# A graph attention kernel: layer 1's transposes and last product in two one-bank PSUM buffers, and the first tile's x multiplied while its rows arrive

## The chip, the cores and the metric

The kernel runs on one core of one Trainium2 chip. Its time is device time in microseconds, as the median of several runs. A profile, taken by the hardware profiler in an execution of its own, gives start and duration of every instruction. TensorE is called PE, VectorE DVE, ScalarE ACT, GpSimd POOL, and the queue that issues most stores SP.

## The reference, cut to what matters

Two graph attention layers on 10,000 nodes with 170,000 edges (self loops included), each followed by a layer norm and a residual product; all in fp32.

```
def gat_conv(x, edge_index, W, a_src, a_dst, bias, heads, out_ch, concat):
    ...
    xl = (x @ W).reshape(n, heads, out_ch)
    alpha_src = jnp.einsum('nhc,hc->nh', xl, a_src)
    alpha_dst = jnp.einsum('nhc,hc->nh', xl, a_dst)
    e = jax.nn.leaky_relu(alpha_src[src] + alpha_dst[dst], 0.2)
    m = jax.ops.segment_max(e, dst, num_segments=n)
    e = jnp.exp(e - m[dst])
    s = jax.ops.segment_sum(e, dst, num_segments=n)
    alpha = e / (s[dst] + 1e-16)
    msg = xl[src] * alpha[:, :, None]
    out = jax.ops.segment_sum(msg, dst, num_segments=n)
    ...
h = gat_conv(x, edge_index, W1, a_src1, a_dst1, b1, HEADS, HID, True)     # 4 heads of 256
h = jax.nn.relu(layer_norm(h, g1, be1))
h = h + (h0 @ Wr1 + br1)                                                   # 768 -> 1024
h1 = h
h = gat_conv(h, edge_index, W2, a_src2, a_dst2, b2, 1, OUT_DIM, False)    # 1024 -> 768
h = layer_norm(h, g2, be2) + (h1 @ Wr2 + br2)
```

The output is the layer norm of x plus this h.

## The kernel before

The nodes are cut into 79 tiles of 128, sorted by their number of edges, so that a tile's nodes need about the same number of neighbour rows. That number is the tile's count of slots. In the order in which the tiles are worked on it climbs from 8 to 26, has one tile of 41 in the middle (tile 39), and falls from 27 to 9 again.

There are three stages. The first (to about 878 us in the profile) multiplies x by W1, writes the result with its attention numbers to `table1` in HBM, and sorts the nodes beside it. Layer 1 (about 881 to 3437 us) gathers rows of `table1`, sums them weighted, and writes `table2`. Layer 2 does the same with `table2`.

Layer 1 is the function `ordered_layer1`. Rows come through a ring of 29 slots (`RING1`) in SBUF, each row filled by a gather that POOL issues (L424); a slot is filled anew when its row has been used. The order of the work on every engine is the order in which the Python code issues it, and the tile framework adds the waits. For tile t one turn of the loop at L742 does the following.

- `weights_of(t)` (L701): DVE computes the attention weights of all slots (L477 to L499), ACT their exp (L485). For the first one to four slots (`on_pe`) ACT makes diagonal matrices (L713) and PE multiplies the rows by them into `acc` (L719), a tile of two PSUM banks. Most of this is issued during the turn before, so that it is ready.
- The other slots: of each four, ACT scales three by their weights (`multiply`, L508) and DVE adds them to `acc` (L515); DVE scales and adds the fourth by itself (L519).
- x of the tile, gathered by POOL into `xt`, is transposed on PE in six blocks (`columns`, L583), copied to `xT` by ACT in two pieces of 512 and 256 columns (L586), and multiplied by Wr1 on PE (`product`, L171) into `r`. SP stores `xt` to `x_d` (L771).
- For the tile before (t - 1): mean and deviation of `acc` on DVE (L561, L563) with the root on ACT (L565), then h on DVE (L574 to L577), its relu and the sum with `r` (L776). PE transposes h in eight blocks (L583), ACT copies them to `hT` in two pieces (L586), and PE multiplies by W2 into `full` (L789): 512 and then 258 columns, 8 steps each. A fp32 matmul of 128x512 shows as two records.
- `store` (L734), one turn later, lets ACT copy `full` to SBUF in one piece of 770 columns (L738), and SP writes it to `table2`.

PE's order within a turn is thus: x's transposes, h's transposes, the product with Wr1, the product with W2, and the next tile's `acc`. ACT's is: the root, the row copy, the first multiplies, xT's copies, more multiplies, hT's copies, the remaining multiplies, and the next tile's exp and diagonals.

x's transposes, h's transposes and `full` take turns in one PSUM buffer of two banks:

```
tc.tile_pool(name="ps_h1", bufs=1, space=PSUM) as ps_big
p = ps_big.tile([P, 2 * BANK], F32, name="big")
```

A new tile of that pool may be written only when all readers of the one before are done. Before the loop the code issues the gathers of tile 0's 8 rows (L685), then x's gather (L692), then the remaining rows of the ring (L693). Tile 0's x goes through PE inside the first turn, after tile 0's `acc`.

Of the kernel before, what the change touches and what calls it, by code (L numbers as in the profile page):

```python
# [28 lines left out]
F32 = mybir.dt.float32  # L29
# [3 lines left out]
OP = mybir.AluOpType  # L33
AX = mybir.AxisListType

P = 128
BANK = 512
# [42 lines left out]
def gnn_kernel(ctx, tc, x, x_cols, src, dst, src_col, dst_col, W1, a_src1, a_dst1, b1, g1, be1, Wr1, br1,  # L80
               W2, a_src2, a_dst2, b2, g2, be2, Wr2, br2, out, n_edges):
    nc = tc.nc
# [3 lines left out]
    C1, C2 = H1 * DH1, H2 * DH2  # L86


    R1, R2 = C1 + 2 * H1 + 1, C2 + 2 * H2
# [74 lines left out]
    def product(aT, w, n, pool=None):  # L164

        k = w.shape[1]
        p = (pool or ps_big).tile([P, 2 * BANK], F32, name="big")
        for c in range(0, n, BANK):
            e = min(n, c + BANK)
            for j in range(k):  # L170
                nc.tensor.matmul(p[:, c:e], aT[:, j, :], w[:, j, c:e], start=(j == 0), stop=(j == k - 1))  # L171
        return p
# [403 lines left out]
        nc.vector.reciprocal(inv, inv)  # L576
        nc.vector.scalar_tensor_tensor(to, to, inv, b, op0=OP.mult, op1=OP.add)  # L577

    def columns(to, a):

        p = ps_big.tile([P, 2 * BANK], F32, name="big").rearrange("p (k n) -> p k n", n=P)
        for i in range(to.shape[1]):
            nc.tensor.transpose(p[:, i, :], a[:, i * P:(i + 1) * P], ident)  # L583

        def move(j, e):
            return lambda: nc.scalar.copy(to[:, j:e, :], p[:, j:e, :])  # L586

        return [move(j, min(j + BANK // P, to.shape[1])) for j in range(0, to.shape[1], BANK // P)]

    def load(s, w):  # L590
        nc.sync.dma_start(s[:, :, :w.shape[1]], w.rearrange("(k p) n -> p k n", p=P))

# [83 lines left out]
        return order[:, TURNS[t]:TURNS[t] + 1]  # L676

    def ordered_layer1():
        nonlocal ps_big
        with tc.tile_pool(name="b1", bufs=1) as pool, tc.tile_pool(name="small1", bufs=2) as small, \  # L680
                tc.tile_pool(name="ps_acc1", bufs=2, space=PSUM) as ps_acc, \
                tc.tile_pool(name="ps_h1", bufs=1, space=PSUM) as ps_big, \
                tc.tile_pool(name="ps_r1", bufs=1, space=PSUM) as ps_r, tc.manual_schedule():
            ring = Ring(pool, table1, R1, RING1, {})
            ring.fetch(SLOTS[0])  # L685

            def fetch_x(t):
                xt = pool.tile([P, D0], F32, name="xt")
                gather(xt, x[:, :], nodes(t))
                return xt  # L690

            xt = fetch_x(0)  # L692
            ring.fetch(RING1)  # L693
# [40 lines left out]
            def store(t):  # L734

                nonlocal full
                row = pool.tile([P, R2], F32, name="row")
                nc.scalar.copy(row, full[:, :R2])  # L738
                full = None
                nc.sync.dma_start(table2[TURNS[t] * P:(TURNS[t] + 1) * P, :], row)  # L740

            for t in range(NT + 1):  # L742
                live, events = t < NT, []
                n = SLOTS[t] if live else 0
                first = done = on_pe(t) if live else 0
                whole = live and n <= ring.size
                if whole and not ready:
                    ahead = weights_of(t)
                    ready += itertools.islice(ahead, 2)

                def multiplied(upto):
                    nonlocal done
                    while whole and done < min(upto, n):
                        if shared(t, done):
                            multiply(ring.slot(FIRST[t] + done), e[:, done], DH1)
                        done += 1

                if whole:
                    e, acc = ready
                if last:  # L760
                    r, means = last
                    stats = deviation(small, pieces(means[:, :C1], BANK))
                for _ in ahead:
                    pass
                if full is not None:
                    store(t - 2)
                moves = []
                if live:
                    xT = pool.tile([P, K0, P], F32, name="xT")
                    moves = columns(xT, xt)  # L770
                    nc.sync.dma_start(x_d[t], xt)  # L771
                multiplied(first + 2)
                if last:
                    h = pool.tile([P, C1], F32, name="h")
                    scaled(h, [means[:, :C1]], stats, g1_b, be1_b)
                    nc.vector.scalar_tensor_tensor(h, h, 0.0, r[:, :C1], op0=OP.max, op1=OP.add)  # L776
                for move in moves:
                    move()
                multiplied(first + LEAD)
                if last:  # L780
                    hT = pool.tile([P, K1, P], F32, name="hT")
                    events = [(first + j, move) for j, move in enumerate(columns(hT, h))]
                if live:
                    r = product(xT, wr1, C1, ps_r)

                def to_layer2():
                    nonlocal full
                    nc.sync.dma_start(h1_d[t - 1], hT.rearrange("p k n -> p (k n)"))
                    full = product(hT, w2, R2)  # L789

                if last:
                    events.append((first + 2, to_layer2))

                def next_x():
                    nonlocal xt
                    xt = fetch_x(t + 1)

                if t + 1 < NT:
                    events.append((first + 2, next_x))

                def due(k):
                    while events and events[0][0] <= k:
                        events.pop(0)[1]()

                if live and not whole:
                    due(n)
                    acc = ps_acc.tile([P, 2 * BANK], F32, name="acc")
                    ad = small.tile([P, H1], F32, name="ad")
                    nc.vector.tensor_copy(ad, ring.slot(FIRST[t])[:, C1:C1 + H1])
                    attend_parts(small, ring, acc, acc, ad, None, H1, DH1, t)  # L810
                ready = []
                ahead = iter(())
# [12 lines left out]
                last = None  # L825
                if live:
                    last = r, acc
# [405 lines left out]
```

## Time and profile before

| what | value |
|---|---|
| median of 3 runs | 5400.24 us (5399.1 to 5413.62) |
| profiled execution | 5617.1 us, span of its instructions 5615.3 us |
| granted PE clock, mean over the span | 0.928 |
| PE busy | 4816.7 us (86% of the span) |
| DVE busy | 4352.5 us (78%) |
| ACT busy | 3154.8 us (56%) |
| POOL busy | 3241.5 us (58%) |
| layer 1: first gather issued, last row copy | 881.41 us, 3436.50 us |
| PE, DVE and ACT busy in layer 1's 957 to 1200 us | 233.7, 217.2 and 194.5 of 243 us |
| share of the DMA engines' time in use, 957 to 1200 and 2600 to 2850 us | 0.88 and 0.99 |

The profile names an instruction by its line, engine and operation, and by the tiles that it writes and reads (out<-in). A line of the timeline has the start in us, the time taken, and, where several like instructions follow one another, their number after an x. In brackets is the time for which the engine stood idle before it, and what ended that. In the lists by line a bar stands ahead of the busy time and the mean in ns, and a second one ahead of the idle time. "issue" is idle time for which the profile shows no cause. A wait for several things is put down to the one that came last.

### The profile page before, as it was taken

Reading aid. Unit: us, or ns where it says so; the run is one execution under the profiler, and the core shown is the slowest. Engines: PE = TensorE matmul, PEld = TensorE weight load, DVE = VectorE, ACT = ScalarE, POOL = GpSimd, SP = SyncE. Lnnn points to the kernel's source line nnn. Section 1 sums busy time; section 2 is a strip of 40 time slices with the busy share of each in tenths; the row PEclk is TensorE's granted clock in tenths of the full one; section 3 lists DMA queues with packets and bytes.
Section 4 is the critical chain, followed back from the end, with each engine's and each line's share of the span. In section 5 each row is a group of like instructions: output and inputs, shape, how many; then the busy total and the mean of one; then the engine's idle time right before and its main releaser. Section 6 shows DMA issues by size and latency. Waiting matters only on the chain. (4 is left out here: it accounts for less than half of the span.)

```text
span 5615.3 us, 59633 instructions
## 1 busy us (share of the span) xinstructions
PE 4816.7 (86%) x15011; PEld 2843.6 (51%) x15011; DVE 4352.5 (78%) x8008; ACT 3154.8 (56%) x8125; POOL 3241.5 (58%) x3159
## 2 busy tenths in 40 slices
PE   9999996999999874789999997988887737788898
PEld 3444443555555542455555554655554524555565
DVE  5783345999998888889999994987777666777787
ACT  3443444888888876788888883443333213333343
POOL 3447455556666555566665542666566566666663
PEclk9999998999999987899999998999898867888999
DMA  4333537899999986899999986999888778888885
GB/s 156 122 98 87 93 96 262 314 332 351 363 365 368 342 323 244 317 350 363 368 355 354 335 296 223 327 329 318 287 310 298 277 260 296 292 314 299 308 331 213
DMA packets 474308, 1591.38 MB, mean 283 GB/s; under 512 B 118327, under 2 KB 122487, under 8 KB 473958
## 3 DMA queue, kind: packets, MB, share of 16 engines
q0 software_dynamic: 322384, 1286.62, 64.1%
q1 hardware_dynamic: 149520, 297.43, 15.7%
q10 hardware_dynamic: 2054, 3.42, 0.2%
q8 instruction: 127, 2.08, 0.1%
q14 instruction: 223, 1.83, 0.1%
HBM read 1431.80 MB, written 177.29 MB: 287 GB/s over the span
## 5 line engine op out<-in xcount | busy, mean ns | idle before, releaser
L424 POOL DMA_INDIRECT ring<-table,slots x2675 | 2660.8, 995 | 1742.0 <-issue 605.0
L519 DVE SCALAR_TENSOR_TENSOR acc<-ring,e,acc 128x256 f32<-128x256 f32 (+1 forms) x2538 | 1571.3, 619 | 120.3 <-PE acc L719 36.8
L508 ACT ACTIVATE ring<-ring,e 128x256 f32<-128x256 f32 x3320 | 1355.9, 513 | 1.4 <-ACT ring L508 1.3
L515 DVE TENSOR_TENSOR acc<-acc,ring 128x1024 f32<-128x1024 f32 x830 | 1021.4, 1231 | 80.7 <-issue 6.7
L890 PE MATMUL big<-wr,w 128*128 128x512 f32 (+1 forms) x2528 | 898.1, 502 | 117.8 <-issue 117.0
L876 PE MATMUL big<-ring,diagonals 128*128 128x256 f32 x2672 | 712.2, 425 | 166.3 <-issue 112.7
L171 PE MATMUL big<-w,xT 128*128 128x512 f32 x1896 | 823.7, 596 | 22.4 <-DMA w<-in_W_dram 9.6
L171 PE MATMUL big<-wr,xT 128*128 128x512 f32 x1896 | 836.1, 598 | 6.6 <-issue 6.6
L171 PE MATMUL big<-w,hT 128*128 128x512 f32 (+1 forms) x2528 | 830.4, 486 | 1.2 <-ACT hT L586 1.2
L890 PEld LDWEIGHTS big<-wr,w 128*128 128x128 f32 x2528 | 493.6, 196 | 493.9 <-issue 461.5
L876 PEld LDWEIGHTS big<-ring,diagonals 128*128 128x128 f32 x2672 | 564.4, 214 | 321.4 <-issue 186.5
L171 PEld LDWEIGHTS big<-w,hT 128*128 128x128 f32 x2528 | 477.8, 189 | 373.9 <-issue 334.6
L875 ACT ACTIVATE diagonals<-ident,e 128x128 f32<-128x128 f32 x1336 | 412.2, 392 | 442.7 <-remote 144.2
L719 PE MATMUL acc<-ring,diagonals 128*128 128x256 f32 x1816 | 443.7, 401 | 229.1 <-ACT diagonals L713 224.5
L171 PEld LDWEIGHTS big<-w,xT 128*128 128x128 f32 x1896 | 361.3, 191 | 480.4 <-issue 461.9
L171 PEld LDWEIGHTS big<-wr,xT 128*128 128x128 f32 x1896 | 357.9, 192 | 428.4 <-issue 428.4
L719 PEld LDWEIGHTS acc<-ring,diagonals 128*128 128x128 f32 x1816 | 360.0, 201 | 305.0 <-ACT diagonals L713 210.1
L565 ACT ACTIVATE sd<-mv,eps 128x1 f32<-128x1 f32 x237 | 70.1, 296 | 570.3 <-issue 242.4
L660 DVE TENSOR_TENSOR scr<-big,ad_b 128x1024 f32<-128x1024 f32 x79 | 96.7, 1225 | 374.0 <-ACT row L657 366.1
L713 ACT ACTIVATE diagonals<-ident,e 128x128 f32<-128x128 f32 x908 | 279.2, 390 | 114.5 <-DVE e L499 76.2
L665 POOL TENSOR_TENSOR row<-row,none 128x1024 f32<-128x1024 f32 x79 | 187.2, 2369 | 258.6 <-ACT row L657 257.9
L663 ACT ACTIVATE scr<-scr 128x256 f32<-128x256 f32 x632 | 254.2, 405 | 120.3 <-DVE scr L660 120.3
(172 smaller groups left out, 3771.1 us busy)
## 6 DMA issues: line engine op xcount, KB each, us to landing
ring<-table,slots POOLq DMA_INDIRECT x2675
table<-row SPq DMA_DIRECT2D x79, 516.0 KB
h_d<-hT SPq DMA_DIRECT2D x79, 512.0 KB
w<-h_d SPq DMA_DIRECT2D x79, 512.0 KB
table<-row SPq DMA_DIRECT2D x79, 385.0 KB
ring<-table SPq DMA_DIRECT2D x79, 385.0 KB
xT<-in_x_cols_dram SPq DMA_DIRECT2D x79, 384.0 KB
x_d<-xt SPq DMA_DIRECT2D x79, 384.0 KB
```

The lines of the kernel that those rows point to most:

```text
L171: nc.tensor.matmul(p[:, c:e], aT[:, j, :], w[:, j, c:e], start=(j == 0), stop=(j == k - 1))
L424: nc.gpsimd.indirect_dma_start(out=to, out_offset=None, in_=table, in_offset=bass.IndirectOffsetOnAxis(ap=index, axis=0), **more)
L508: nc.scalar.activation(row[:, s], row[:, s], AF.Copy, scale=e[:, h:h + 1])
L515: nc.vector.tensor_add(acc[:, :c], acc[:, :c], row[:, :c])
L519: nc.vector.scalar_tensor_tensor(acc[:, s], row[:, s], e[:, h:h + 1], (acc if first is None else first)[:, s], op0=OP.mult, op1=OP.add)
L663: nc.scalar.activation(m[:, s], m[:, s], AF.Copy, accum_out=row[:, C1 + i * H1 + h:C1 + i * H1 + h + 1])
L665: nc.gpsimd.tensor_add(row[:, :C1], row[:, :C1], b1_b)
L713: nc.scalar.activation(diagonals[:, k * H1 + i, :], ident, AF.Copy, scale=e[:, k, i:i + 1])
L719: nc.tensor.matmul(acc[:, c:d], diagonals[:, k * H1 + i, :], ring.slot(FIRST[t] + k)[:, c:d], start=(k == 0 and c % BANK == 0), stop=(k == ...
L875: nc.scalar.activation(diagonals[:, k % G, :], ident, AF.Copy, scale=e[:, k, :])
L876: nc.tensor.matmul(to, diagonals[:, k % G, :], ring.slot(FIRST[t] + k)[:, ON_PE2:C2], start=False, stop=(k == n - 1), skip_group_check=True)
L890: nc.tensor.matmul(r[:, c:d], hT[:, j, :], wr2[:, j, c:d], start=False, stop=(j == K1 - 1 and (d < C2 or not whole(t))), skip_group_check= ...
```

## The change

It replaces `columns` by `halves` and adds `from_x`. The pool `ps_h1` now has two buffers of one bank each in place of one of two banks. The transposes of x go into one buffer (four blocks) and the other (two blocks), those of h likewise (four and four), and the product with W2 too: 512 columns in one, 258 in the other. Each ACT copy then belongs to one buffer, and `store` makes two copies. For tile 0, x's gather is issued ahead of all rows, and x's transposes, copies, its store to `x_d` and its product with Wr1 are issued ahead of the loop, so on PE ahead of tile 0's `acc` and on ACT ahead of tile 0's exp. `r` of the tile before gets a name of its own. The arithmetic stays the same.

```diff
-    def columns(to, a):
-
-        p = ps_big.tile([P, 2 * BANK], F32, name="big").rearrange("p (k n) -> p k n", n=P)
-        for i in range(to.shape[1]):
-            nc.tensor.transpose(p[:, i, :], a[:, i * P:(i + 1) * P], ident)
-
-        def move(j, e):
-            return lambda: nc.scalar.copy(to[:, j:e, :], p[:, j:e, :])
-
-        return [move(j, min(j + BANK // P, to.shape[1])) for j in range(0, to.shape[1], BANK // P)]
...
-                tc.tile_pool(name="ps_h1", bufs=1, space=PSUM) as ps_big, \
+                tc.tile_pool(name="ps_h1", bufs=2, space=PSUM) as ps_half, \
                 tc.tile_pool(name="ps_r1", bufs=1, space=PSUM) as ps_r, tc.manual_schedule():
             ring = Ring(pool, table1, R1, RING1, {})
-            ring.fetch(SLOTS[0])
...
+            def halves(to, a):
+
+
+                moves, per = [], BANK // P
+                for j in range(0, to.shape[1], per):
+                    m = min(per, to.shape[1] - j)
+                    p = ps_half.tile([P, BANK], F32, name="half").rearrange("p (k n) -> p k n", n=P)
+                    for i in range(m):
+                        nc.tensor.transpose(p[:, i, :], a[:, (j + i) * P:(j + i + 1) * P], ident)
+                    moves.append(lambda j=j, m=m, p=p: nc.scalar.copy(to[:, j:j + m, :], p[:, :m, :]))
+                return moves
+
+            def from_x(t):
+
+                xT = pool.tile([P, K0, P], F32, name="xT")
+                moves = halves(xT, xt)
+                nc.sync.dma_start(x_d[t], xt)
+                return xT, moves
 
             xt = fetch_x(0)
             ring.fetch(RING1)
...
                 row = pool.tile([P, R2], F32, name="row")
-                nc.scalar.copy(row, full[:, :R2])
+                for c, q in full:
+                    nc.scalar.copy(row[:, c:c + q.shape[1]], q)
                 full = None
                 nc.sync.dma_start(table2[TURNS[t] * P:(TURNS[t] + 1) * P, :], row)
 
+
+            xT, moves = from_x(0)
+            for move in moves:
+                move()
+            r = product(xT, wr1, C1, ps_r)
             for t in range(NT + 1):
...
-                    r, means = last
+                    r_before, means = last
...
-                if live:
-                    xT = pool.tile([P, K0, P], F32, name="xT")
-                    moves = columns(xT, xt)
-                    nc.sync.dma_start(x_d[t], xt)
+                if live and t:
+                    xT, moves = from_x(t)
...
-                    nc.vector.scalar_tensor_tensor(h, h, 0.0, r[:, :C1], op0=OP.max, op1=OP.add)
+                    nc.vector.scalar_tensor_tensor(h, h, 0.0, r_before[:, :C1], op0=OP.max, op1=OP.add)
...
-                    events = [(first + j, move) for j, move in enumerate(columns(hT, h))]
-                if live:
+                    events = [(first + j, move) for j, move in enumerate(halves(hT, h))]
+                if live and t:
                     r = product(xT, wr1, C1, ps_r)
...
-                    full = product(hT, w2, R2)
+                    full = []
+                    for c in range(0, R2, BANK):
+                        q = ps_half.tile([P, BANK], F32, name="half")[:, :min(BANK, R2 - c)]
+                        for j in range(K1):
+                            nc.tensor.matmul(q, hT[:, j, :], w2[:, j, c:c + q.shape[1]],
+                                             start=(j == 0), stop=(j == K1 - 1))
+                        full.append((c, q))
```

More of the change, by code (lines that the diff above doesn't have):

```diff
@@ L678, in ordered_layer1 @@
     def ordered_layer1():
-        nonlocal ps_big
         with tc.tile_pool(name="b1", bufs=1) as pool, tc.tile_pool(name="small1", bufs=2) as small, \
                 tc.tile_pool(name="ps_acc1", bufs=2, space=PSUM) as ps_acc, \
-                tc.tile_pool(name="ps_h1", bufs=1, space=PSUM) as ps_big, \
+                tc.tile_pool(name="ps_h1", bufs=2, space=PSUM) as ps_half, \
                 tc.tile_pool(name="ps_r1", bufs=1, space=PSUM) as ps_r, tc.manual_schedule():
             ring = Ring(pool, table1, R1, RING1, {})
-            ring.fetch(SLOTS[0])
             def fetch_x(t):
```

## The prediction

> **What bounds the kernel now.** The change touches layer 1 alone, which runs from 881 to 3437 us of the profiled span. I read three views: busy time by stage, then who waited for whom in layer 1, then the timelines of one tile. The first, its columns being the time and number of instructions of TensorE (PE), its weight loads, VectorE (DVE), ScalarE (ACT) and GpSimd, then clock, DMA share and GB/s:
>
> ```profile
> 957.00:1200.00 243.00, 233.71 (x777) 135.68 (x775) 217.21 (x365) 194.53 (x451) 128.92 (x129) 1.00 0.88 314
> 1640.00:2600.00 960.00, 733.05 (x2407) 445.50 (x2406) 836.32 (x1335) 767.54 (x1893) 570.37 (x565) 0.90 0.89 329
> 2850.00:3220.00 370.00, 349.47 (x1158) 205.37 (x1158) 343.34 (x577) 305.64 (x731) 219.60 (x217) 0.99 0.95 346
> ```
>
> PE looks like the bound: 233.71/243 = 96%, DVE 89%. The gaps decide otherwise. A tile of 12 slots, PE, ACT and DVE:
>
> ```profile
> 1012.63 1.89 PE L719 MATMUL acc<-ring,diagonals 128*128 128x256 f32 x8
> 1014.36 0.82 PE L583 MATMUL big<-ident,xt 128*128 128x128 f32 x6
> 1016.18 1.09 PE L583 MATMUL big<-ident,h 128*128 128x128 f32 x8 [1.00 <-ACT xT L586]
> 1012.87 0.80 ACT L738 COPY row<-big 128x770 f32<-128x770 f32 x1 [2.65 <-PE big L171]
> 1013.57 1.71 ACT L508 ACTIVATE ring<-ring,e 128x256 f32<-128x256 f32 x4
> 1015.27 0.86 ACT L586 COPY xT<-big 128x512 f32<-128x512 f32 x2
> 1014.56 2.06 DVE L519 SCALAR_TENSOR_TENSOR acc<-ring,e,acc 128x256 f32<-128x256 f32 x4 [0.55 <-PE acc L719]
> ```
>
> PE has one pause a tile, the 1.00 us in brackets: the transposes of h wait until both copies have emptied the buffer. All else on PE is back to back, so it reaches L583 every 25.13 us (to 1039.48). But DVE waits only 0.55 us for PE here, and in a tile of 15 slots not at all:
>
> ```profile
> 1199.47 1.22 DVE L776 SCALAR_TENSOR_TENSOR h<-h,big 128x1024 f32<-128x1024 f32 x1
> 1200.61 2.06 DVE L519 SCALAR_TENSOR_TENSOR acc<-ring,e,acc 128x256 f32<-128x256 f32 x4
> 1200.84 1.07 PE L583 MATMUL big<-ident,h 128*128 128x128 f32 x8 [1.08 <-ACT xT L586]
> ```
>
> There PE's transposes of h start 0.15 us after DVE has written h (1199.47 + 1.22 = 1200.69), whatever the copies did. Going tile by tile through both timelines, PE's period is 25.13 us for 12 or 13 slots, 26.87 for 14 or 15, 28.60 for 16 or 17, 30.33 for 18; DVE's, less its waits, is 24.7, 26.0, 26.2, 28.3, 28.35, 29.7 and 29.9 for 12 to 18 slots. So PE leads by at most 0.7 us, with 12, 14, 16 or 18 slots; with 13, 15, 17, 19 and more, DVE or the rows' arrival does. What DVE waits in 957 to 3400 us, in total, times and longest:
>
> ```profile
> DVE acc L519 <- PE acc L719: 36.8, 42, 5.3
> DVE e L477 <- DMA ring<-table,slots: 27.2, 12, 5.1
> ```
>
> 36.8 us in 77 tiles is the most that a faster PE could give back inside the layer, and much of it is not PE's own: in the tiles of 19 to 27 slots PE itself stands waiting for ACT's diagonals (L713).
>
> **What the Trainium skill says.** "Perfetto Trace Analysis", section Identifying the Most-Contended Engine: matmul busy share is a poor measure of the tensor engine's closeness to its limit, occupancy a fair one for VectorE. The trace agrees: 96% busy, yet PE follows DVE with 15 slots. Same page, Optimizing Tensor Performance: "Independent matmul groups should rotate through different PSUM banks so the ACT/DVE evacuation of one overlaps the next group's matmuls". The 1.00 us pause is what its absence costs here. "PSUM — Partial Sum Buffer", section on bank collisions: two engines may use different banks at once; the trace of before never shows ACT reading one half while PE fills the other. "TensorE: Matmul & The Clock Gate", Part 1: after an idle window PE runs at half clock for some 3.4 us; here, after 5.75 us idle, six transposes took 1.52 us and not 0.82.
>
> **The change part by part.**
>
> *Transposes in halves.* h's first four transposes now need only the first xT copy, and that copy only the first four x-transposes. Those end 2 x 0.137 us before the sixth (0.82/6 each), at T+0.55 from the group's start T. ACT must be free: today its four multiplies end at 1015.28 = T+0.92; the row copy ahead of them shrinks from 0.80 to a second piece of 258 columns (the 256-column xT copy takes 0.37), so they end near T+0.5. First copy T+0.64 to T+1.22 (the 512-column copy takes 0.58), h from T+1.27, today T+1.82: **0.55 us off PE's period**, pause 1.00 to 0.45. The second copy ends T+1.5, before the fifth h-transpose at T+1.8, so no new pause. Bounds: 0.28 if ACT is late (two copies instead of one awaited), 0.7 if the multiplies end sooner.
>
> *The product in halves.* The same 16 matmuls (32 records). ACT's row copy 0.80 becomes two, like xT's pair: 0.86, so +0.06 x 79 = 5 us of ACT, hidden by its idle 2.65 us here; were ACT the bound, 5 us lost. The first is done while PE fills the other bank.
>
> *What DVE can use of 0.55.* Its first waits from tile 2 are 5.35, 1.33, 0.55, 0.42, 0, 0, 0.23, 0.57, 0.29, then 0 in tiles 11 to 21. Letting PE gain 0.55 a tile on top of the 1.1 below, I carried both periods on: PE is ahead of DVE from tile 5 (2.7 us gained), and tiles 8 to 10 give their 0.23 + 0.57 + 0.29 = 1.1: **3.8 us** by tile 11. Tiles 22 to 24 and 54 to 57 (18 slots) wait 0.33 to 0.55, of which 0.33 also stands in the tiles of 19, where PE isn't the cause: 0.5 us in all. Elsewhere nothing: DVE and DMA (0.99 busy at 369 GB/s in 2600 to 2850) are next.
>
> *First tile.* x's gather is issued first, and its transposes, copies and product (1.5 + 0.9 + 12.85 us, cold) move ahead of the rows' diagonals on PE, and its copies ahead of the first exp on ACT. On GpSimd's queue the first eight rows come one issue later, 1.25 us; x's store to x_d on SP's queue comes earlier. x is first behind two 512 KB loads, so it lands near 888 (1.4 MB at 387 GB/s, plus 2 to 3 us as the later gathers show); the product ends near 904, when the first diagonals are ready (now 903.37 for PE). One thing the trace leaves untold: today ACT's copies begin at 914.38, 6.0 us after the transposes' recorded end (906.92 + 1.49). If that stall comes again it delays the product to 910. That is still harmless: DVE needs 18.3 us of work from its first sum to tile 0's h (907.16 to 936.91 less 11.4 idle), PE can't take h before 937, so DVE may start as late as 918. But none of it passes tile 1:
>
> ```profile
> 926.07 0.97 POOL L424 DMA_INDIRECT xt<-in_x_dram,order  x1 [0.31 <-issue]
> 935.34 1.52 PE L583 MATMUL big<-ident,xt 128*128 128x128 f32 x6 [5.75 <-issue]
> ```
>
> The next x is the 35th gather; GpSimd issues one each 1.25 to 1.3 us and the DMA engines are full (1.00, 387 GB/s in 900 to 950), so it still lands near 935, and PE starts from there as before. What is left is the finer copy in tile 1, at cold clock: **1.1 us**, in the 3.8 above. Bounds: -3 to +5.
>
> *The end.* No next tile hides PE here:
>
> ```profile
> 3399.01 0.82 PE L583 MATMUL big<-ident,xt 128*128 128x128 f32 x6
> 3412.06 10.51 PE L171 MATMUL big<-w,hT 128*128 128x512 f32 x32
> 3423.51 1.09 PE L583 MATMUL big<-ident,h 128*128 128x128 f32 x8 [0.94 <-ACT row L738]
> 3425.81 10.62 PE L171 MATMUL big<-w,hT 128*128 128x512 f32 x32 [1.21 <-ACT hT L586]
> 3436.50 0.80 ACT L738 COPY row<-big 128x770 f32<-128x770 f32 x1 [10.75 <-PE big L171]
> ```
>
> Tiles 76 to 78 are PE's: 3 x 0.55 = 1.65. The 0.94 goes (the first half is free already), 1.21 falls to 0.2 (four transposes run beside the first copy), the last copy from 0.80 to 0.37: 1.65 + 0.94 + 1.0 + 0.43 = **4.0 us**, all on the path, since layer 2's gathers wait for the last table2 row.
>
> Sum: 3.8 + 0.5 + 4.0 = 8.3 us. The profiled execution took 5617.1 us (span 5615.3): 5608.8 for its like. The unprofiled median is 5400.24; the stages concerned follow DVE and PE, so I take off the same: **5392**. About 0.3% (16 us) is what a measurement of this kernel can tell from no change.
>
> **Rivals.** *PE is the bound after all.* For: 96% busy, a pause in nearly every tile. Against: DVE's missing waits. Then 64 pauses (the count of L583's waits for xT's copies) x 0.55 = 35 us: 5365, or part of it. *Nothing arrives*: the copies come no earlier because ACT is late, and the start is eaten by the wait at 935: 5400. *Waits inside the groups*: PE now has four new waits a tile, at the bank borders of transposes and product. If each empties its pipeline and costs a matmul's slot of 0.43 us, PE's period grows by 4 x 0.43 - 0.55 = 1.2 us; that is felt in the 23 tiles of 12, 14, 16 and 18 slots (28 us) and hardly elsewhere, less 3 us kept at the end: 5425. It decides from 0.14 us a wait (no gain) and is slower by 0.3% from about 0.35. Against it: L719's matmuls wait four times for ACT and still run eight records in 1.89 us.
>
> **How the numbers follow.** Forecast 0.60, own range 5384 (every wait for PE with 12 to 18 slots and at the end falls, 16 us) to 5398 (little but the last copies). PE the bound 0.17, nothing 0.16, waits in the groups 0.07. The range 5378 to 5405 holds the first and third and the milder part of the second. Faster by over 0.3%: 0.17 + 0.03 of the forecast's tail = 0.20; slower 0.07; within 0.73.
>
> **What would show it.** In the changed profile: the pause before h's transposes at 0.3 to 0.5 us; DVE's waits for acc in tiles 3 to 10 near nothing, its tile periods with 15 and 17 slots still 28.3 and 29.7; tile 1's x-transposes again near 935; from the last x-transposes to the end of the last row copy 2.9 us less than now (3399.01 to 3437.30). Wrong if DVE's periods themselves shrink, if tile 1 starts well away from 935, or if gaps appear inside PE's groups.

## The result and the profile after

The changed kernel takes 5388.17 us (median of 20 runs, 5380.39 to 5396.90), the kernel before 5397.51 in the same series: a ratio of 0.998, with a 95% interval of 0.9974 to 0.9987, so 7 to 14 us less, 9.3 by the medians. The forecast was 8.3 us.

The profiled execution of after took 5386.19 us, against 5617.1 for the profile of before that the prediction rests on. Most of that difference isn't the change: from the last row copy of layer 1 to the end there are 1951 us in one and 2178 in the other, all in layer 2. A second profile of before, taken later on another chip (`before_again` below), took 5388.63 us and has 1947 there; in layer 1 as a whole it agrees with the first within 1 us (2555.9 and 2556.8 us from the first gather to the end of the last row copy), though not in every part of it. Times of single tiles are counted from that first gather below.

Busy time by stage in after, the same three stretches as before (they begin 7.3 us later here, since the first stage ended later; columns as before):

```profile
964.00:1207.00 243.00, 235.73 (x781) 136.80 (x780) 221.23 (x370) 201.04 (x478) 134.32 (x132) 0.99 0.90 320
1647.00:2607.00 960.00, 739.67 (x2416) 452.32 (x2415) 837.95 (x1337) 767.58 (x1921) 572.33 (x566) 0.88 0.90 329
2857.00:3227.00 370.00, 349.04 (x1167) 205.80 (x1166) 343.81 (x578) 304.57 (x743) 217.89 (x216) 1.00 0.97 347
```

Only the first stretch is fuller: all three engines do 1 to 4% more in the same time, as they must where tiles follow faster. In the other two DVE and ACT moved by less than 0.5%; PE is busy for 1% more in the second, at a clock of 0.88 in place of 0.90. The timeline of the tile of 12 slots that the prediction took apart, PE, ACT and DVE:

```profile
1014.89 1.89 PE L725 MATMUL acc<-ring,diagonals 128*128 128x256 f32 x8
1016.62 0.82 PE L687 MATMUL half<-ident,xt 128*128 128x128 f32 x6
1017.95 1.09 PE L687 MATMUL half<-ident,h 128*128 128x128 f32 x8 [0.51 <-ACT xT L688]
1015.09 0.38 ACT L745 COPY row<-half 128x258 f32<-128x258 f32 x1 [1.83 <-PE half L803]
1015.36 1.71 ACT L508 ACTIVATE ring<-ring,e 128x256 f32<-128x256 f32 x4
1017.31 0.86 ACT L688 COPY xT<-half 128x512 f32<-128x512 f32 x2 [0.24 <-PE half L687]
1016.82 2.06 DVE L519 SCALAR_TENSOR_TENSOR acc<-ring,e,acc 128x256 f32<-128x256 f32 x4 [0.24 <-PE acc L725]
```

The pause before h's transposes is 0.51 us where it was 1.00, and PE's period 24.64 where it was 25.13. Of the row copy only the 258-column piece is left ahead of the multiplies; ACT now waits 0.24 us for the first four transposes, so the copy couldn't come much sooner. DVE's wait for acc fell from 0.55 to 0.24. And with 15 slots (the timeline around h of tile 10, DVE and PE):

```profile
1199.80 1.22 DVE L786 SCALAR_TENSOR_TENSOR h<-h,big 128x1024 f32<-128x1024 f32 x1
1200.94 2.06 DVE L519 SCALAR_TENSOR_TENSOR acc<-ring,e,acc 128x256 f32<-128x256 f32 x4
1201.17 1.74 PE L687 MATMUL half<-ident,h 128*128 128x128 f32 x8 [2.00 <-DVE h L786]
```

PE is further ahead and simply waits longer for DVE's h: 2.00 us instead of 1.08. The gain has gone into a wait. Over the whole of layer 1 past the start (964 to 3408 us), DVE's two waits, in total, times and longest:

```profile
DVE acc L519 <- PE acc L725: 35.2, 39, 3.8
DVE e L477 <- DMA ring<-table,slots: 27.5, 15, 4.7
```

They were 36.8 and 27.2 in the first profile of before, and 41.5 and 27.3 in before_again. PE's idle time ahead of h's transposes fell from 89 and 90 us in the two profiles of before to 63 (in 52 of the 79 turns the pause is now 0.51 us; in others PE waits for something else). Of these 26 to 28 us DVE got back 1.6 by the first profile and 6.3 by the second.

The end of layer 1, PE and ACT:

```profile
3398.21 0.82 PE L687 MATMUL half<-ident,xt 128*128 128x128 f32 x6
3410.77 10.51 PE L803 MATMUL half<-w,hT 128*128 128x512 f32 x32
3421.11 1.28 PE L687 MATMUL half<-ident,h 128*128 128x128 f32 x8
3422.43 10.61 PE L803 MATMUL half<-w,hT 128*128 128x512 f32 x32
3429.65 0.58 ACT L745 COPY row<-half 128x512 f32<-128x512 f32 x1 [6.63 <-PE half L803]
3433.08 0.37 ACT L745 COPY row<-half 128x258 f32<-128x258 f32 x1 [2.85 <-PE half L803]
```

Here no pause is left: the brackets of 0.94 and 1.21 us on PE are gone, and one copy of 0.37 us stands behind the last product instead of 0.80. From the last x-transposes to the end of the last row copy it is 35.2 us (3398.21 to 3433.45), before 38.3, and 40.0 in before_again, where the last product took 12.31 us and not 10.62.

### The profile page after: what moved, and what is told of

It is laid out like the page before. It is cut to its first block, busy times and chain, and to the rows that moved or that the text cites. A ratio compares the mean times of both kernels' runs of the same rounds, so it can differ in the third digit from the quotient of the medians.

```text
span 5384.3 us, 59633 instructions
## 1 busy us (share of the span) xinstructions
PE 4721.3 (88%) x15011; PEld 2818.7 (52%) x15011; DVE 4348.2 (81%) x8008; ACT 3138.9 (58%) x8204; POOL 3238.2 (60%) x3159
## 5 line engine op out<-in xcount | busy, mean ns | idle before, releaser
L906 PE MATMUL big<-wr,w 128*128 128x512 f32 (+1 forms) x2528 | 846.4, 488 | 0.0
L892 PE MATMUL big<-ring,diagonals 128*128 128x256 f32 x2672 | 667.2, 412 | 193.3 <-ACT diagonals L891 180.3
L803 PE MATMUL half<-w,hT 128*128 128x512 f32 (+1 forms) x2528 | 830.4, 486 | 0.0
L892 PEld LDWEIGHTS big<-ring,diagonals 128*128 128x128 f32 x2672 | 548.2, 208 | 309.8 <-ACT diagonals L891 211.8
L803 PEld LDWEIGHTS half<-w,hT 128*128 128x128 f32 x2528 | 477.8, 189 | 372.7 <-issue 310.7
L906 PEld LDWEIGHTS big<-wr,w 128*128 128x128 f32 x2528 | 482.6, 191 | 340.1 <-issue 307.5
L891 ACT ACTIVATE diagonals<-ident,e 128x128 f32<-128x128 f32 x1336 | 400.5, 387 | 147.6 <-DVE e L499 129.3
L719 ACT ACTIVATE diagonals<-ident,e 128x128 f32<-128x128 f32 x908 | 278.5, 387 | 117.6 <-DVE e L499 117.6
```

Of the source, the lines that this page charges most:

```text
L719: nc.scalar.activation(diagonals[:, k * H1 + i, :], ident, AF.Copy, scale=e[:, k, i:i + 1])
L803: nc.tensor.matmul(q, hT[:, j, :], w2[:, j, c:c + q.shape[1]], start=(j == 0), stop=(j == K1 - 1))
L891: nc.scalar.activation(diagonals[:, k % G, :], ident, AF.Copy, scale=e[:, k, :])
L892: nc.tensor.matmul(to, diagonals[:, k % G, :], ring.slot(FIRST[t] + k)[:, ON_PE2:C2], start=False, stop=(k == n - 1), skip_group_check=True)
L906: nc.tensor.matmul(r[:, c:d], hT[:, j, :], wr2[:, j, c:d], start=False, stop=(j == K1 - 1 and (d < C2 or not whole(t))), skip_group_check= ...
```

## The experiments

When DVE has finished h of a tile, in us after the first gather of layer 1 (one profile each), and the end of the last row copy:

| kernel | h of tile 1 | 4 | 11 | 22 | 57 | 75 | last row copy |
|---|---|---|---|---|---|---|---|
| before, first profile | 77.5 | 157.9 | 347.5 | 667.2 | 1969.5 | 2468.2 | 2555.9 |
| before_again | 77.6 | 158.1 | 347.8 | 667.4 | 1968.7 | 2467.4 | 2556.8 |
| after | 75.0 | 152.8 | 340.8 | 661.1 | 1962.4 | 2461.0 | 2544.7 |
| halves_only | 76.1 | 154.6 | 342.0 | 661.6 | 1967.8 | 2467.0 | 2550.6 |
| first_only | 76.1 | 155.6 | 345.3 | 665.4 | 1971.4 | 2470.6 | 2558.0 |
| less_dve | 75.8 | 153.3 | 339.4 | 651.2 | 1957.1 | 2440.7 | 2524.3 |
| less_pe | 74.7 | 152.0 | 339.5 | 660.2 | 1980.5 | 2478.8 | 2563.8 |
| after_again (second chip) | 82.1 | 160.3 | 348.3 | 671.7 | 1985.0 | 2483.4 | 2566.7 |
| x_first (second chip) | 79.5 | 158.0 | 345.5 | 667.8 | 1973.0 | 2473.2 | 2556.8 |
| warm_pe (second chip) | 82.0 | 159.1 | 346.7 | 667.1 | 1978.9 | 2477.3 | 2560.6 |
| start_order (second chip) | 91.7 | 167.0 | 354.8 | 675.1 | 1986.6 | 2486.3 | 2569.6 |
| share5 | 75.2 | 152.7 | 338.5 | 652.6 | 1951.0 | 2440.5 | 2524.0 |
| both | 75.8 | 153.1 | 339.0 | 653.1 | 1951.3 | 2440.7 | 2524.3 |
| x_first_both | 76.6 | 155.1 | 342.9 | 656.8 | 1952.5 | 2442.7 | 2526.0 |

Outside the tiles of 19 slots and more (25 to 53) the steps from tile to tile repeat within some tenths of a microsecond; inside, profiles of like kernels differ by up to 5 us. Medians of different series are compared below through the kernel before of the same series, and the profiles' layer 1 is given beside them.

### First series: the parts, and what bounds (before: 5394.23 us)

**halves_only**: the two buffers without the first tile's new order.

```diff
+            ring.fetch(SLOTS[0])
...
-            xT, moves = from_x(0)
-            for move in moves:
-                move()
-            r = product(xT, wr1, C1, ps_r)
...
-                if live and t:
+                if live:
                     xT, moves = from_x(t)
...
-                if live and t:
+                if live:
                     r = product(xT, wr1, C1, ps_r)
```

> The two one-bank buffers alone; the first tile's x stays inside the first turn, after tile 0's acc, and tile 0's rows are issued ahead of x. As the prediction has it, this is the whole change: about 8 us faster than before (pause 0.5 us shorter in tiles 1 to 4 and 8 to 10, 3 us at the end). The other reading, from the trace of after: tile 1 starts there 1.7 us earlier and its product is 1.4 us shorter, both from the first tile's new order, so the halves alone bring only 5 to 7 us and the rest is the first tile's. If PE were the bound, some 35 us.

5390.82 us, ratio 0.999 (0.9983 to 0.9996). In the table it is 5.8 us ahead of before at tile 11, the changed kernel 7.0. So it has most of the start, and the same end (83.7 us from h of tile 75 to the last row copy, before 87.7 and 89.4). Between tiles 22 and 75 it gave 5.5 us back, nearly all of it in the tiles of 19 slots and more.

**first_only**: the kernel before with the first tile's new order (the same lines the other way round, with `columns`).

> The first tile's new order alone, with the one two-bank buffer and the one row copy of before. The prediction: nothing (0, bounds -3 to +5), since tile 1's x sets PE's start. The other reading: 3 us faster, 1.7 from the earlier landing of tile 1's x and 1.4 from its product running at a higher clock, since DVE waits for acc for 7 us in all in tiles 2 to 5 and so takes every microsecond that PE gains there. Pause before h as before, 1.0 us.

5394.20 us, ratio 0.9996 (0.9988 to 1.0005): nothing that can be told by the time, as the prediction had it. The trace shows a gain all the same: 2.5 us at tile 4, kept to tile 22, and then lost in the tiles of 19 slots and more. By the medians the two parts, 3.4 and 0.0 us, don't add up to the 9.3 of the whole change; their intervals (2 to 9 us less, and 6 us less to 3 us more) are wide enough for it. At tile 4 of the profiles they do: 3.5 and 2.5 us, the whole change 5.3.

**less_dve**: one DVE operation less in the turns of tiles 12 to 74, so that h stays unscaled there.

```diff
-    def scaled(to, parts, mean_and_deviation, g, b):
+    def scaled(to, parts, mean_and_deviation, g, b, short=False):
...
-        nc.vector.scalar_tensor_tensor(to, to, inv, b, op0=OP.mult, op1=OP.add)
+        if not short:
+            nc.vector.scalar_tensor_tensor(to, to, inv, b, op0=OP.mult, op1=OP.add)
...
-                    scaled(h, [means[:, :C1]], stats, g1_b, be1_b)
+                    scaled(h, [means[:, :C1]], stats, g1_b, be1_b, short=12 <= t <= 74)
```

> The changed kernel less one DVE operation of 1.28 us (the scaling of h by its deviation and the sum with be1, so h is left unscaled) in the turns of tiles 12 to 74. If DVE is the bound there: the tiles of 13, 15 and 17 slots (17 of these tiles) get 1.2 us shorter each, those of 16 and 18 slots (14) by 0.3 until PE binds, 25 us in all below the changed kernel, and up to 34 if the tiles of 19 follow. If PE is the bound: within 3 us of the changed kernel.

5362.84 us, ratio 0.9935 (0.9921 to 0.9949): 31 us below before, where the changed kernel was 9 below, so 22 us between them (in layer 1 of the profiles 20.4). That is near the 25 us which the DVE theory gave as its lower number. With 15 slots the mean period fell from 28.3 to 27.0 us. With 16 slots it only fell from 28.5 to 28.0, because now PE binds, as the timeline of DVE in such a tile shows:

```profile
3011.69 1.22 DVE L787 SCALAR_TENSOR_TENSOR h<-h,big 128x1024 f32<-128x1024 f32 x1
3013.93 2.06 DVE L519 SCALAR_TENSOR_TENSOR acc<-ring,e,acc 128x256 f32<-128x256 f32 x4 [1.01 <-PE acc L726]
```

From tile 22 to 57 it gained nothing (1305.9 us, before 1301.3 to 1302.3), though DVE has some 45 us less to do there. DVE's waits in 957 to 3400 us say why:

```profile
DVE acc L519 <- PE acc L726: 97.4, 50, 5.2
DVE e L477 <- DMA ring<-table,slots: 29.2, 16, 4.5
```

The waits for rows stayed (27.5 in after), those for acc rose from 35.2. In tiles 23 to 57 alone the latter went from 27.6 to 79.6 us. In the tiles of 19 slots and more a chain sets the pace at this point: DVE's weights (L499), ACT's diagonals from them, PE's acc, and only then DVE's first sum. From the end of the weights to that sum it is never under 8.42 us, in after as in less_dve. DVE has at least 8.1 us of other work in that time in after and 6.7 in less_dve, so the operation saved only lengthens the wait.

**less_pe**: half of the last product left out in the turns of tiles 12 to 74.

```diff
-                        for j in range(K1):
+                        steps = K1 // 2 if 12 <= t <= 74 else K1
+                        for j in range(steps):
                             nc.tensor.matmul(q, hT[:, j, :], w2[:, j, c:c + q.shape[1]],
-                                             start=(j == 0), stop=(j == K1 - 1))
+                                             start=(j == 0), stop=(j == steps - 1))
```

> The changed kernel with half of the last product's steps left out (4 of 8, so the product is over half of h) in the turns of tiles 12 to 74: PE has 5.2 us less work a tile. If DVE and the rows are the bound: 0 to 10 us below the changed kernel, since DVE's waits for acc in these tiles sum to some 28 us, most of them behind ACT's diagonals. If PE is the bound: 5.2 x 63, some 300 us below it, or as much of it as DVE allows.

5399.17 us, ratio 1.0008 (1.0000 to 1.0017). Some 330 us of work taken from PE, and the kernel is 5 us above before, where the changed one was 9 below: 14 us *slower* (in layer 1 of the profiles 19). Where tiles have 12 to 18 slots nothing moved: 498.3 us from tile 57 to 75, in after 498.7, and 320.7 from tile 11 to 22, in after 320.3. So the amount of PE's work isn't the bound. Neither theory had a loss; it lies between tiles 22 and 57, and the timeline shows where it comes from. PE and DVE in two tiles of 19 slots, first in less_pe:

```profile
1680.98 5.34 PE L804 MATMUL half<-w,hT 128*128 128x512 f32 x16
1692.14 10.12 PE L725 MATMUL acc<-ring,diagonals 128*128 128x256 f32 x32 [5.83 <-ACT diagonals L719]
1702.30 2.06 DVE L519 SCALAR_TENSOR_TENSOR acc<-ring,e,acc 128x256 f32<-128x256 f32 x4 [2.61 <-PE acc L725]
```

and in after:

```profile
1697.72 3.73 PE L725 MATMUL acc<-ring,diagonals 128*128 128x256 f32 x16 [0.90 <-ACT diagonals L719]
1701.82 3.73 PE L725 MATMUL acc<-ring,diagonals 128*128 128x256 f32 x16 [0.37 <-ACT diagonals L719]
1705.59 2.06 DVE L519 SCALAR_TENSOR_TENSOR acc<-ring,e,acc 128x256 f32<-128x256 f32 x4 [0.33 <-PE acc L725]
```

PE is done early and then stands idle for 5.83 us until ACT has the diagonals. That costs its clock: the 32 records take 10.12 us instead of 7.8 (with the 0.37 between the halves). acc is late, and DVE waits 2.61 us instead of 0.33. The Trainium skill, "TensorE: Matmul & The Clock Gate", Part 1, has the reason: the clock is judged in free-running windows of some 3.4 us, and after an idle one it is half. The trace agrees in part: its stretches of half clock are multiples of 3.41 us, and between 960 and 3400 us they sum to 205 us in before_again, 239 in after and 519 in less_pe. But here shorter pauses than such a window were enough, and not always: 2.29 us ahead of acc cost the clock at 1797.56 us in after, 2.38 at 2594.83 did not, nor did 3.26 at 1864.81 in before_again. In tiles 23 to 57 DVE's waits for acc sum to 50.2 us in less_pe and 27.6 in after, its waits for rows (L477) to 26.2 and 29.8: 19 us more in all, which is what less_pe lost between tiles 22 and 57 (1320.3 us, after 1301.3).

The same thing, small, is seen in the changed kernel itself: in after, PE waits 2.3 to 3.9 us ahead of acc in turns 29, 30, 31, 47 and 50, acc takes 8.9 us or more there, and DVE's wait at tiles 30, 31, 32, 48 and 51 is 1.37 to 1.74 us instead of 0.33. In before_again only one of these five is above 0.6. That the change causes it isn't shown: in the second profile of the changed kernel (after_again, below) only two of the five are, and in tiles 23 to 57 DVE's waits for acc sum to 27.6 and 28.3 us in the two, in before_again to 29.6. In halves_only and first_only they sum to 37.0 and 33.9, and both lost 5 us there.

### Second series: the start, and the clock (before: 5654.49 us)

These four ran on another chip, where every kernel takes some 260 us longer, most of it in layer 2. Their times are compared only with the runs of before beside them. For single tiles there is no profile of before from this series; the first profile of before, whose layer 2 is as long (2178 us, here 2197 to 2212), stands in for it.

**after_again**: the changed kernel, unchanged.

> The changed kernel once more, unchanged, as the yardstick of this series and for a second profile of it. From the first profile: layer 1's stretch from first gather to last row copy 2544.7 us there, 2555.9 before. If what differs between executions in the tiles of 19 slots and more is chance, the second profile differs there by a few us either way, and tiles 1 to 22 and 58 to 78 agree within 0.5 us. Time: 9 us below before.

5654.10 us, ratio 0.9995 (0.9980 to 1.0009): on this chip the change brings nothing. The profile says where the start went; DVE, in tile 0:

```profile
905.43 0.19 DVE L499 TENSOR_TENSOR e<-e,total 128x32 f32<-128x32 f32 x1
924.98 2.07 DVE L519 SCALAR_TENSOR_TENSOR acc<-ring,e,acc 128x256 f32<-128x256 f32 x4 [19.35 <-remote]
```

DVE waits 19.35 us for a sum that PE had recorded as done by 908.1. Of PE's signals the trace holds few in this time, at 910.20, 915.78, 921.41, 924.91 and 924.95, and DVE starts 0.03 us after the last; in after the four signals of the same group are 0.43 us apart. So tile 0's first sum starts 41.9 us after the first gather (25.0 in after), and h of tile 1 ends at 82 instead of 75 us. The 6.0 us stall of ACT in the first profile of before may be the same thing; before_again doesn't have it. Why the signals come so late there isn't settled.

**x_first**: x's gather first, its product back inside the first turn (as halves_only, without the first added line).

> The changed kernel with x's gather ahead of tile 0's rows, but tile 0's transposes, copies and product left inside the first turn, after its acc. If the first tile's gain (2.3 us by tile 4) comes from tile 1's x landing sooner, it stays: h of tile 4 some 5 us earlier than before, as in the changed kernel. If it comes from work moved out of PE's way (PE takes tile 0's product before its acc and stands free when tile 1's x lands, at a lower clock), it goes: 3.3 us as with the halves alone. Time: between 0 and 2 us above the changed kernel.

5644.12 us, ratio 0.9982 (0.9973 to 0.9991), and 2.3 us ahead of after_again at tile 4, 0.1 us behind the first profile of before. Neither reading: on this chip the three kernels that multiply tile 0's x ahead of its acc all finish h of tile 0 at 60 us, this one at 57.4, and the first profile of before has 55.5. So what that product's place is worth here hangs on the stall; these runs don't separate the two further.

**warm_pe**: work for PE where it stands idle.

```diff
+            def again(t):
+
+                return 2 if t in (29, 30, 31, 48, 49, 50) else 4 if 32 <= t <= 47 else 0
...
+                        for _ in range(again(t) if c == 0 else 0):
+                            nc.tensor.matmul(q, hT[:, 0, :], w2[:, 0, c:c + q.shape[1]], start=True, stop=True)
                         for j in range(K1):
```

> The changed kernel with work added to PE that changes no result: the first step of the last product is done 2 more times in turns 29 to 31 and 48 to 50 (1.7 us of PE each) and 4 more times in turns 32 to 47 (3.5 us). PE stands idle there for 2 to 12 us ahead of the next tile's acc. If that idle time costs PE its clock, so that acc takes 8.9 us instead of 7.8 and DVE waits 1.37 us for it instead of 0.34, the added work pays: DVE's waits at tiles 30, 31, 32, 48 and 51 fall back to 0.34, some 5 us below the changed kernel. If the rows' arrival sets these tiles anyway: within 2 us of it. If PE were the bound there: 22 turns x 1.7 to 3.5, some 66 us above it.

5645.15 us, ratio 0.9985 (0.9974 to 0.9997). DVE's waits for acc at tiles 29 to 53 fell from 26.3 us in after_again to 21.9, and the stretches of half clock from 239 us to 167. So PE's idle time does cost its clock, and some 66 us of added PE work cost nothing. Whether the 4.4 us reach the end can't be told: the two intervals overlap.

**start_order**: in tile 1's turn, h of tile 0 and its product ahead of tile 1's x.

```diff
-                if live and t:
+                if live and t > 1:
                     xT, moves = from_x(t)
-                multiplied(first + 2)
+                multiplied(n if t == 1 else first + 2)
...
-                if live and t:
+                if live and t > 1:
                     r = product(xT, wr1, C1, ps_r)
...
+                if t == 1:
+                    for _, move in events:
+                        move()
+                    events = []
+                    to_layer2()
+                    store(0)
+                    xT, moves = from_x(1)
+                    for move in moves:
+                        move()
+                    r = product(xT, wr1, C1, ps_r)
+                elif last:
```

> The changed kernel with another order in the turn of tile 1 alone: h of tile 0, its product with W2 and its row copies go ahead of tile 1's x on PE and ACT, and all ACT multiplies of tile 1 ahead of both, since PE now stands idle for 12 us ahead of tile 1's x with h of tile 0 ready for 8 of them. If PE's chain after tile 1's x (h, two products, acc of tile 2) is what the start waits for, it gets 11 us shorter, DVE's waits of 8.36 and 3.8 us shrink, and the start gains 4 to 5 us. If the landing of the rows is: nothing, or some us lost to the cold clock.

5660.74 us, ratio 1.0005 (0.9991 to 1.0020), and 6.8 us behind after_again at tile 4. A miss: on this chip h of tile 0 came at 60 us, when tile 1's x had landed (PE has it at 56.2 in after_again), so x only waited behind it, until 78.5. On a chip where h of tile 0 is ready at 44 us it wasn't tried.

### Third series: before again, and a better version (before: 5395.87 us)

**before_again**: the kernel before, unchanged.

> The kernel before once more, unchanged, for a profile of it beside this series. In the first series h of tile 4 was done 152.8 us after the first gather in the changed kernel, 154.6 with the halves alone and 155.6 with the first tile alone; the profile shown of before says 157.9, but its executions are 220 us longer elsewhere. If the change's gain at the start is real, this profile has 157 to 158 on a chip like the first series', and its ACT or DVE shows no stall of 5 us or more in tile 0 that the changed kernel is spared. If the gain was such a stall, it has 153 to 155 there.

5395.63 us, ratio 1.0001. h of tile 4 at 158.1 us and no stall: the gain at the start is real. PE in the turn of tile 1 and POOL's gather for it, before_again:

```profile
936.79 1.51 PE L583 MATMUL big<-ident,xt 128*128 128x128 f32 x6 [13.51 <-DMA xt<-in_x_dram,order]
939.58 1.97 PE L583 MATMUL big<-ident,h 128*128 128x128 f32 x8 [1.28 <-ACT xT L586]
941.35 12.36 PE L171 MATMUL big<-wr,xT 128*128 128x512 f32 x24
927.51 0.97 POOL L424 DMA_INDIRECT xt<-in_x_dram,order  x1 [0.30 <-issue]
```

and after:

```profile
941.00 1.51 PE L687 MATMUL half<-ident,xt 128*128 128x128 f32 x6 [12.14 <-DMA xt<-in_x_dram,order]
942.76 1.97 PE L687 MATMUL half<-ident,h 128*128 128x128 f32 x8 [0.25 <-ACT xT L688]
944.53 10.90 PE L171 MATMUL big<-wr,xT 128*128 128x512 f32 x24
931.72 0.97 POOL L424 DMA_INDIRECT xt<-in_x_dram,order  x1 [0.30 <-issue]
```

With the first gather at 882.70 and 888.74, x of tile 1 is issued 44.8 and 43.0 us after it and reaches PE at 54.1 and 52.3: 1.8 us. The pause falls from 1.28 to 0.25: 1.0 us. The product takes 1.5 us less, because PE's clock is back at full 56.7 us after the first gather and not at 62.4. Together 4.3 us, which the next x-transposes show (82.9 and 78.6 us). Not all of the 1.8 us need come from x's new place: halves_only, which has the old one, gets x of tile 1 at 53.1 us.

**share5**: `SHARE = 4` becomes `SHARE = 5`, so ACT scales four rows of five.

> The changed kernel with ACT scaling four rows of five in place of three of four (one number): in the tiles of 15 to 19 slots DVE has one scaled sum of 2.06 us less and one plain sum of 1.24 us more, 0.82 us less a tile, and ACT 1.7 us more. If DVE is the bound: 16 tiles of 15 and 17 slots give 0.82 us each, 14 of 16 and 18 some 0.3 until PE binds, 18 us below the changed kernel, up to 23 with the tiles of 19. If PE is the bound: within 3 us of the changed kernel. If ACT becomes it: slower.

5362.46 us, ratio 0.9942 (0.9927 to 0.9956): 33 us below before, so 24 below the changed kernel (in layer 1 of the profiles 20.7), close to the 18 to 23 of the DVE theory. The end of h in two tiles that follow each other, the second of 15 slots, in after:

```profile
3054.33 1.22 DVE L786 SCALAR_TENSOR_TENSOR h<-h,big 128x1024 f32<-128x1024 f32 x1
3082.65 1.22 DVE L786 SCALAR_TENSOR_TENSOR h<-h,big 128x1024 f32<-128x1024 f32 x1
```

and in share5:

```profile
3058.53 1.22 DVE L786 SCALAR_TENSOR_TENSOR h<-h,big 128x1024 f32<-128x1024 f32 x1
3085.61 1.22 DVE L786 SCALAR_TENSOR_TENSOR h<-h,big 128x1024 f32<-128x1024 f32 x1
```

That is 27.08 us where it was 28.32. On the mean the period fell by 1.05 us with 15 slots, 0.6 with 16 and with 17, 0.3 with 18. ACT, busy for 82% of the last of the three stretches in after and for 89% of it here, keeps up.

**both**: SHARE = 5 and warm_pe's added work.

> The changed kernel with ACT scaling four rows of five, and with the added PE work of the last series in the tiles of 20 slots and more. The two touch different tiles, so they should add up: 18 us from the first and 5 us from the second (9 by the medians of the last series, with wide intervals), 23 to 27 us below the changed kernel. If the rows set the tiles of 20 and more: 18.

5355.20 us, ratio 0.9926 (0.9913 to 0.9939), the fastest of all: 41 us below before. Its five runs (5353.09 to 5357.34 us) all lie below share5's five (5358.15 to 5371.37), but layer 1 took as long in both profiles, 2524.3 and 2524.0 us, so where the difference comes from isn't known. DVE's waits for acc and for rows, 957 to 3400 us, in share5:

```profile
DVE acc L519 <- PE acc L725: 36.2, 40, 2.8
DVE e L477 <- DMA ring<-table,slots: 29.3, 15, 4.5
```

and in both:

```profile
DVE acc L519 <- PE acc L725: 31.4, 41, 2.7
DVE e L477 <- DMA ring<-table,slots: 33.8, 19, 5.0
```

4.8 us less waiting for acc again, and 4.5 us more waiting for rows: in these tiles the rows' arrival is the next limit, right behind the chain.

**x_first_both**: both, with tile 0's product inside the first turn.

> As the one before, with tile 0's x still gathered first, but transposed and multiplied inside the first turn. On the chip of the second series leaving it there was worth 7 us of median and 2.2 us of start; if that holds, 2 to 7 us below the one before. If the first series' chip tells (the first tile's move as a whole 1.8 us at the start), 0 to 2 us above it.

5363.19 us, ratio 0.9938 (0.9924 to 0.9952), and 2.0 us behind both at tile 4, 1.7 at the end of layer 1 (one profile each; by the medians it is 8 us, with intervals that overlap). On a chip without the stall the product ahead of tile 0's acc seems to pay, as the second of the two readings had it.

## Why the prediction was right, point by point

- **DVE or the rows bind, not PE**: right for the tiles of 12 to 18 slots, and the ground of the forecast. One operation less on DVE gave 22 us and one scaled sum less a tile 24, while leaving out half of PE's last product moved whole rows of these tiles (11 to 22, 57 to 75) by 0.4 us at most. Their periods with 15 and 17 slots stayed at 28.3 and 29.7 us. From 19 slots on it is not so simple: the chain from DVE's weights over ACT's diagonals and PE's acc sets the pace, with the rows close behind. A shorter pause before h doesn't shorten that chain, since PE waits for the diagonals there anyway, so the forecast of no gain from these tiles holds.
- **Pause 1.00 to 0.45**: 0.51, so 0.49 us a tile and not 0.55: the first xT copy starts 0.69 us after the transposes do, and not 0.64. The matmul groups have no new gaps (1.09, 10.51 us as before), so the rival of waits at bank borders is out. What the prediction missed in the trace of before, ACT reading one bank while PE fills the other, is there in after, in 147 of the 474 copies of layer 1.
- **Row copies at +0.06 us hidden**: right. In 69 of the 79 tiles the two run back to back, in 0.84 us on the mean where the one copy took 0.79.
- **Start and tiles to 11, 3.8 us**: mis-sized, 7.0 measured against before_again. The step that failed is "it still lands near 935", with "what is left is the finer copy in tile 1": x of tile 1 reached PE 1.8 us sooner and its product was 1.5 us shorter. Both lie within the bound of +5 that the text set for this part. In before_again POOL waits for landed rows from 26 to 38 us after the first gather, once for 1.67 us; in after it waits for a row at none of these issues. Why is open. The rest came as computed: DVE's waits in tiles 2 to 10 shrank from 9.1 to 5.0 us, in tiles 11 to 21 nothing was to be had.
- **The untold stall**: harmless at 6 us, as argued (h of tile 0 at 55.5 and 46.1 us in the two profiles of before, h of tile 1 at 77.5 and 77.6). The text gave 918 as the latest start of DVE, 36.6 us after the first gather; at 41.9, in after_again, the start was lost.
- **Tiles of 18 slots, 0.5 us**: there, as far as profiles can tell. The seven steps sum to 212.3 and 212.2 us before, 211.6 in after, 211.5 in halves_only and 212.2 in first_only.
- **The end, 4.0 us**: from h of tile 75 to the last row copy 4.0 against the first profile of before (87.7 to 83.7), 5.7 against before_again, whose last product ran slower; halves_only has 83.7 too, first_only 87.4. From the last x-transposes on 3.05 against the first profile, with 2.9 foretold; tiles 76 to 78 gave the rest.

By the profiles the sum is 11 to 12 us, by the medians 9.3. That the medians came within 1 us of the forecast is in part luck: the start was worth nearly twice what was foretold, and the medians show less than the profiles do. Open is what moves the tiles of 19 slots and more by up to 5 us between profiles of like kernels; DVE's waits for acc carry it (37.0 and 33.9 us in halves_only and first_only, 27.6 to 29.6 in after and before_again), and that spread is as large as half of the effect.

## What to carry to other kernels

A second buffer shortens a pause on the engine that has it, but the time is worth only what the engine that sets the pace was waiting for. Look for tiles in which that engine waits for nothing: there the half microsecond just becomes a longer wait elsewhere. At the ends, where nothing overlaps, the same half microsecond counts in full; and the better move is to take work off the engine that binds (here one number, SHARE, was worth 24 us on top of the change's 9). And ask where in a tile the saved work stood: in the tiles of 19 slots and more less_dve's saving stood beside a chain over ACT and PE, and was lost.

## What was not expected of the hardware

- Less work on PE made the kernel slower: after more idle time ahead of a group of 32 records (5.83 us in the tile shown) PE did it in up to 10.1 us instead of 7.8, and DVE waited 2.3 us longer. Pauses of 2 to 3 us did so in some turns and not in others. Repeating a product's first step to fill such gaps cost no time that was seen.
- On one chip, with the DMA engines in use for 0.96 of the time at the start of layer 1, PE's signals are recorded 5.6 us apart and DVE started 17 us after PE's last recorded matmul for it. In before_again, with 1.00 there, and in after it started at once. A change of the start's order that gains 2 us on one chip can lose it on another (x_first_both against both, x_first against after_again; one profile each).
